# Softmax weights of two batches transposed by TensorE instead of by VectorE and DMAs

## The chip, the cores and the metric

The kernel runs on one core of a Trainium2 chip. The metric is the time of one execution in device microseconds; the number quoted for a kernel is the median of several executions. Besides these there is one execution under the hardware profiler, whose instructions can be read one by one; "the span" is the time from its first to its last instruction.

## What is computed

The input is 64 batches of 128 tokens with 512 features. Each batch goes through one multi-query attention layer and gets the result added:

```python
xn   = layernorm(x, g_in)
q    = (xn @ Wq) * DH**-0.5          # 16 heads of 64
k, v = split(xn @ Wkv)               # one head of 64, shared by all query heads
k, v = concat(null_k, k), concat(null_v, v)      # one extra "null" key
sim  = q @ k.T + concat(null_bias, attn_bias)    # 128 queries x 129 keys
sim  = where(causal or padding mask, -big, sim)
out  = softmax(sim) @ v
x    = x + layernorm(out @ Wo, g_out)
```

All of it is float32.

## The kernel before

The order of the work is written out by hand: the kernel is one long function `step(n)`, called for n = -6 to 62, and each engine executes its own instructions in the order in which `step` issues them. There is no planner. In step n, batch n is at the product of softmax weights and values, batch n+1 at its exponentials, batch n+2 at its scores, batch n-1 at its output projection, and the queries of a group of four later batches are being computed, one quarter per step. Steps up to n = 0 fill this pipeline. The steps that matter here are n = -1, 0 and 1.

**The queries** of groups 1 and later are computed by a scheme with seven products per feature block (`product(g, f, k, ...)`, line 422 in the profile: tiles `pa`, `pw`, `pc`, in PSUM). Products 1, 6, 7 and 4 use the bank `a` one after the other, and ScalarE copies the bank away between them (`keep`, line 433, tiles `kp`, `ku`; `q_out`, line 440 on ScalarE, line 443 on VectorE, tile `qT`). Product 4 and product 3 of a feature block are issued early in the next step (`last`).

**The scores** of a batch (`scores`, line 495, tile `ps`) are computed in two halves: half 0 has the first 64 queries and 64 keys, half 1 has the other 64 queries and 128 keys. Partitions 0 to 63 hold 64 queries of the heads with u = 0, partitions 64 to 127 the same 64 queries of the heads with u = 1, and eight heads lie side by side. The matmuls are 64x64, four of them in the four quarters of the array, and the two halves of its rows write to different banks. Both halves share one two-bank PSUM tile, which is free again when VectorE has added it to bias and mask (`scores_add`, line 508) in the SBUF tile `s`. GpSimd has put bias and mask there before (`bias_add`, line 466; `null_copy`, line 475). There are two such tiles, so batch b+2 takes the one of batch b, and `bias_add(b+2)` waits until batch b's softmax weights have been read for the last time.

**The softmax**: VectorE finds the maxima (line 513), ScalarE computes exponentials and sums head by head (`exps`, line 522), VectorE the reciprocals of the sums (line 539), and GpSimd multiplies by them (`scale`, line 543).

**The transpose.** For the product with the values, the keys have to lie on the partitions. `blocks_T` (line 575) lets VectorE transpose the weights inside blocks of 32x32 into the SBUF tile `sb`, and `blocks_move` (line 601) issues 14 DMAs that carry the blocks to their places in the SBUF tile `aTb`. For all but batch 0 and the last one, the DMAs are issued by SyncE (SP). Batch 0 has its blocks transposed at the end of step -1; 7 of its DMAs are issued by SP there, and 7 by ScalarE in step 0, between the copy `kp` and the addition that `q_out` does. Batch 1 has its blocks transposed in step 0, and its 14 DMAs are issued by SP later in that step, ahead of the four transfers of `tokens_in` (line 295), the loads of `loads_late` and others. `aTb` is shared by all batches but the last eight, and the parts that causality leaves empty were cleared once.

**Values and output**: `values` and `values_end` (line 610, tiles `po`, in the two buffers of the PSUM pool `w`) multiply `aTb` with the values; ScalarE copies the result to SBUF (line 654, tile `oT`). Batch 0 is projected with eight plain matmul steps (`out_mm`, line 669, tile `py`), the following ones in pairs (line 719). `out_stats` computes the output's layer norm.

The PSUM banks `X` and `Y` (pool `ps_y`) belong to the paired output projection. Their first use in the kernel before is in step 2.

The lines around the edits, in step n = 0 and at the end of step n = -1:

```python
product(qg, f, 1, ps_q, "a")
keep("a", "p1")
if n == 0:
    blocks_move(0, take=1)
q_out(qg, f, lo_t, "w", "p1")
```

Of the kernel before, what the change touches and what calls it, by code (L numbers as in the profile page):

```python
# [8 lines left out]
FP = mybir.dt.float32  # L9
# [8 lines left out]
def kernel(  # L18
# [59 lines left out]
    nc = tc.nc  # L78
    B, N, DIM = x.shape
    H = attn_bias.shape[0]  # L80
    DH = w_kv.shape[1] // 2
    P = 128
# [7 lines left out]
    Q = 32  # L90
    NQ = P // Q
    NF = NC // 2
    R8 = 2 * NF
    NL = DH
    ROW = 1 + NL + N + 1
    LK, UK = slice(1, 1 + NL), slice(1 + NL, 1 + NL + N)
# [8 lines left out]
    ps_s = ctx.enter_context(tc.tile_pool(name="ps_s", bufs=1, space=PSUM))  # L105
    ps_q = ctx.enter_context(tc.tile_pool(name="ps_q", bufs=1, space=PSUM))
    ps_y = ctx.enter_context(tc.tile_pool(name="ps_y", bufs=1, space=PSUM))
# [105 lines left out]
    ident = const.tile([P, P], FP, name="ident")  # L213
# [10 lines left out]
    aTb = const.tile([P, 6, R8, Q], FP, name="aTb")  # L224
# [181 lines left out]
    def product(g, f, k, pool, tag, start=True):  # L406

        if start:
            prod[tag] = pool.tile([P, HT], FP, tag=tag, name=f"p{tag}_{g}_{f}_{k}")
        lo, hi = xT[g][:, 0 : GB // 2], xT[g][:, GB // 2 :]  # L410
        t1, t2, t3, t4 = (xS.get((g, i)) for i in range(1, 5))
        w, t = {
            1: (a11, lo[:, :, lo_k]),
            2: (a12, lo[:, :, hi_k]),
            3: (s4, hi[:, :, hi_k]),
            4: (a22, t4),
            5: (s1, t1),
            6: (s2, t2),
            7: (s3, t3),
        }[k]  # L420
        for kc in range(HK):
            nc.tensor.matmul(  # L422
                prod[tag],
                w[:, kc, f * P : (f + 1) * P],
                t[:, :, kc, :],
                start=(start and kc == 0),
                stop=(kc == HK - 1),
                skip_group_check=not start,
            )

    def keep(tag, name):
        kept[name] = bp.tile([P, HT], FP, tag=f"k{name}", name=f"k{name}", bufs=1)
        nc.scalar.copy(kept[name], prod[tag])  # L433

    def q_out(g, c, toks, tag, name=None):
        lo = toks.start // N
        o = q_part(g, c, lo, lo + 2)
        p = prod[tag].rearrange("p (t h i) -> p t h i", t=2, h=2)
        if name is None:
            nc.scalar.copy(o, p)  # L440
        else:
            k = kept.pop(name).rearrange("p (t h i) -> p t h i", t=2, h=2)
            nc.vector.tensor_tensor(o, p, k, ALU.add)  # L443


    S, nmax, rsum = {}, {}, {}
# [13 lines left out]
    def bias_add(b):  # L460
        g, t = divmod(b, GB)
        if b == B3 + 1:
            S[b] = gp.tile([P, R8, ROW], FP, tag="xT", name=f"s_{b}")
        else:
            S[b] = sp.tile([P, R8, ROW], FP, tag="s", name=f"s_{b}")
        nc.gpsimd.tensor_tensor(  # L466
            S[b][:, :, 1 : ROW - 1],
            biasp,
            mneg[g][:, t].unsqueeze(1).broadcast_to([P, R8, NL + N]),
            ALU.add,  # L470
        )

    def null_copy(b):
        g, t = divmod(b, GB)
        nc.gpsimd.tensor_copy(  # L475
            S[b][:, :, 0 : ROW : ROW - 1],
            nv[g][:, t, DH:].rearrange("p (k e) -> p e k", k=2),
        )
# [85 lines left out]
    def aT_of(b):  # L564
        return aTbs[b % 2 if b >= B2 else 0]

    def blocks_T(b):

        if b > B3 and b % 2:
            if not sb2:  # L570
                sb2.append(gp.tile([P, 6, R8, Q], FP, tag="qT", name="sb2"))
            sb = sb2[0]
        else:
            sb = hp.tile([P, 6, R8, Q], FP, tag="sb", name=f"sb_{b}", bufs=1)
        nc.vector.transpose(  # L575
            sb.rearrange("p j e q -> p e j q"),
            S[b][:, :, 1 : ROW - 1].rearrange("p e (j k) -> p e j k", k=Q),
        )
        sbs[b] = sb

    def blocks_move(b, take=None):

        sb = sbs[b] if take == 0 else sbs.pop(b)
        count = 0
        for u in range(2):
            for i in range(2):
                src = slice((2 * u + i) * Q, (2 * u + i + 1) * Q)
                for j in range(3 + i):
                    count += 1
                    if take is not None and count % 2 != take:  # L590
                        continue
                    dst = slice(j * Q, (j + 1) * Q)
                    jL = j - 2 * u
                    jU, iU = 2 + j, 2 + 2 * u + i
                    if 0 <= jL <= i:

                        js, is_ = slice(jL, jU + 1, jU - jL), slice(i, iU + 1, iU - i)
                    else:
                        js, is_ = slice(jU, jU + 1), slice(iU, iU + 1)
                    queue = nc.scalar if take == 1 else nc.sync  # L600
                    queue.dma_start(  # L601
                        out=aT_of(b)[dst, is_].rearrange("p s e q -> p s (e q)"),
                        in_=sb[src, js].rearrange("p s e q -> p s (e q)"),
                    )

    pos = {}

    def value_mm(b, u, half, keys, vals, slots, start=True):
# [54 lines left out]
    def out_mm(b):  # L663
        pool, tag = ps_w, "w"
        if b > P_LAST:
            pool, tag = (ps_q, "c") if b == P_LAST + 2 else (ps_y, "XY"[b % 2])
        py = pool.tile([P, DIM], FP, tag=tag, name=f"py_{b}")
        for c in range(NC):
            nc.tensor.matmul(  # L669
                py, oT[b][:, c, :], wo[:, c, :], start=(c == 0), stop=(c == NC - 1)  # L670
            )
        ys[b] = py
# [21 lines left out]
    def out_sums(p):  # L694

        yS[p] = bp.tile([P, HC, N], FP, tag="yS", name=f"yS_{p}", bufs=1)
        h11, h12 = oT[p][:, lo_c], oT[p][:, hi_c]
        h21, h22 = oT[p + 1][:, lo_c], oT[p + 1][:, hi_c]
        nc.gpsimd.tensor_tensor(yS[p], h21, h22, ALU.add)
        nc.gpsimd.tensor_tensor(h21, h11, h21, ALU.subtract)  # L700
        nc.gpsimd.tensor_tensor(h11, yS[p], h11, ALU.subtract)
        nc.gpsimd.tensor_tensor(h12, h12, h11, ALU.subtract)
# [69 lines left out]
    def out_stats(b):  # L772
        st = small.tile([P, 6], FP, tag="st", name=f"sto_{b}")
        nc.vector.bn_stats(st, ys[b])
        mv = small.tile([P, 2], FP, tag="mvo", name=f"mvo_{b}")
        nc.vector.bn_aggr(mv, st)
        rstd = small.tile([P, 1], FP, tag="rstdo", name=f"rstdo_{b}")
        nc.vector.tensor_scalar(rstd, mv[:, 1:2], EPS, None, ALU.add)
        nc.gpsimd.tensor_tensor(rstd, rstd, nhalf, ALU.pow)
        y = hp.tile([P, DIM], FP, tag="y", name=f"y_{b}", bufs=3)  # L780
        nc.vector.scalar_tensor_tensor(
            y, ys.pop(b), mv[:, 0:1], gob, ALU.subtract, ALU.mult
        )
        if b == B - 1:

            nc.vector.scalar_tensor_tensor(y, y, rstd, res.pop(b), ALU.mult, ALU.add)
        else:
            yr[b] = y, rstd
        ys[b] = y
# [50 lines left out]
    def step(n):  # L840
        def ok(b, end=B):
            return 0 <= b < end
# [4 lines left out]
        q, f = ok(qg, NG), part  # L847
# [17 lines left out]
        nb = n + 2 if n < B3 - 1 else n + 3  # L865
# [5 lines left out]
        if second:  # L871
            if n != B3 + 1:
                out_sums(p5673)
        elif ok(nb) and n >= 0:
            bias_add(nb)
            null_copy(nb)
        if third:
# [18 lines left out]
        if one:  # L896
            out_mm(n - 1)
            if n == 1:
                out_stats(0)
        if fast:  # L900
            if f == 0:
# [80 lines left out]
        if fast:  # L982
            product(qg, f, 1, ps_q, "a")
            keep("a", "p1")
            if n == 0:
                blocks_move(0, take=1)
            q_out(qg, f, lo_t, "w", "p1")
        if soft and not second:
            exps(eb, 1, 6)
# [52 lines left out]
            scores_max(nb, 0)  # L1042
        if one and n > 1:
            out_stats(n - 1)
        if n == 0:
            blocks_T(1)
        if not ok(n) and fast:
            product(qg, f, 6, ps_q, "a", start=False)
            keep("a", "u2")
# [65 lines left out]
        if ok(mk) and not ok(mkv):  # L1115
            kT_out(mk, k_T(mk))
        if n == -1:
            blocks_T(0)
            blocks_move(0, take=0)
        if n == B3 - 2:  # L1120
            bias_add(B3 + 1)
            null_copy(B3 + 1)
# [49 lines left out]
    for n in range(-6, B - 1):  # L1172
        step(n)
        if n == -6:
            for kc in range(2):
                weights_kv(kc)
            for kc in range(2, KC):
                weights_kv_prod(kc)
            load_late()
        if n == -5:  # L1180
            for kc in range(2, KC):
                weights_kv(kc)
            causal(0)
            mask_neg(0)
            weight_sums()
# [49 lines left out]
```

## Time and profile before

| what | value |
|---|---|
| median of 3 executions | 1135.81 us (1134.92 to 1136.13) |
| the profiled execution | 1134.49 us |
| its span | 1132.7 us |
| TensorE (PE) busy, share of the span | 1084.5 us, 96% |
| VectorE (DVE) busy | 807.5 us, 71% |
| GpSimd (POOL) busy | 745.9 us, 66% |
| ScalarE (ACT) busy | 678.5 us, 60% |
| mean granted TensorE clock | 0.995 |
| busiest DMA queue, q1, share of 16 engines | 40.3% |

In the lines of the profile, a number at the start of a line is the time from the span's start in microseconds, and the next one a duration. "PE L610 ... [4.39 <-DMA aTb<-sb]" means that TensorE sat idle for 4.39 us before this instruction of line 610, and that a DMA from `sb` to `aTb` ended the wait. "SPq" and "ACTq" are the instruction queues of SP and ScalarE when they issue DMAs. A float32 matmul is recorded as two instructions, a transpose as one, so a half of scores, 16 matmuls, shows as x32. Matmuls overlap: a group's duration is a little longer than the distance to the start of the next group, and the distance is what counts in a sum.

### The profile page before, as it was taken

The numbers are of one execution on the slowest core, as the hardware profiler recorded it, in microseconds if no ns is written. First come the engines' busy times: TensorE is split into PE (matmuls) and PEld (weight loads), VectorE is DVE, ScalarE is ACT, GpSimd is POOL, SyncE is SP. The second block draws the span as 40 slices with busy tenths as digits, with TensorE's granted clock in tenths as the row PEclk, the third lists the DMA queues.
The fourth block names the chain that finished last, engine by engine and source line by source line (L and its number), as shares of the span: only waits on it lengthen the run. The fifth ranks groups of instructions, "written<-read, shape, count | busy, mean of one in ns | idle before, by whom it ended". The sixth has DMA issues, their size and how long they took to land.

```text
span 1132.7 us, 27381 instructions
## 1 busy us (share of the span) xinstructions
PE 1084.5 (96%) x9700; PEld 869.1 (77%) x9700; DVE 807.5 (71%) x1737; ACT 678.5 (60%) x2710; POOL 745.9 (66%) x588
## 2 busy tenths in 40 slices
PE   6877999999999999999999999999999999999897
PEld 4454788888878888888888888888888888887642
DVE  6563677776787777788777778877777886666762
ACT  2344656566756656675666667666666755657661
POOL 5444877767665676857577686757767675676742
PEclk9998999999999999999999999999999999999999
DMA  6314234353453435335353533534353353422333
GB/s 184 123 37 126 73 123 118 93 167 100 126 127 120 115 98 163 103 125 135 104 135 97 164 106 122 136 116 121 97 164 107 120 136 112 103 73 72 95 97 107
DMA packets 109591, 131.39 MB, mean 116 GB/s; under 512 B 29712, under 2 KB 74256, under 8 KB 107664
## 3 DMA queue, kind: packets, MB, share of 16 engines
q1 hardware_dynamic: 107776, 127.95, 40.3%
q10 hardware_dynamic: 1680, 1.71, 0.5%
q8 instruction: 77, 1.26, 0.5%
q14 instruction: 58, 0.48, 0.1%
HBM read 54.86 MB, written 31.46 MB: 76 GB/s over the span
## 4 chain that ended last, share of the span: by engine, by line
PE 71%; POOL 7%; DVE 6%; DMA 6%; SPq 4%; issue 2%; ACT 2%; ACTq 1%; POOLq 0%; DVEq 0%
PE pa L422 15%; PE pyX L719 14%; PE pc L422 7%; PE ps L495 7%; PE pyY L719 7%; PE po L610 7%; PE pk L308 4%; PE pw L422 4%; PE pyw L719 3%; DMA x<-in_x_dram 3%; SPq L601 3%; PE py L669 2%; POOL s L466 2%; POOL xS L404 1%; POOL s L543 1%
## 5 line engine op out<-in xcount | busy, mean ns | idle before, releaser
L522 ACT ACTIVATE s<-s,nmax 128x65 f32<-128x65 f32 (+1 forms) x1024 | 372.1, 368 | 1.3 <-DVE nmax L513 0.9
L466 POOL TENSOR_TENSOR s<-biasp,mneg 128x1536 f32<-128x1536 f32 x64 | 221.1, 3455 | 108.3 <-DVE sb L575 105.1
L543 POOL TENSOR_TENSOR s<-s,rinv 128x512 f32<-128x512 f32 (+1 forms) x128 | 189.4, 1481 | 125.7 <-DVE nmro L761 88.6
L654 ACT ACTIVATE oT<-po,nv 128x512 f32<-128x512 f32 x128 | 81.1, 684 | 210.9 <-PE po L610 210.9
L522 ACT ACTIVATION_READ_ACCUMULATOR s<-s,nmax 128x1 f32 x1024 | 194.7, 190 | 0.0
L719 PE MATMUL pyX<-wT,oT 128*128 128x256 f32 x696 | 164.6, 379 | 1.1 <-DVE kyu L731 1.1
L719 PEld LDWEIGHTS pyX<-wT,oT 128*128 128x128 f32 x696 | 132.0, 190 | 19.8 <-DVE kyu L731 1.5
L508 DVE TENSOR_TENSOR s<-ps,s 128x512 f32<-128x512 f32 (+1 forms) x128 | 121.4, 949 | 14.8 <-PE ps L495 12.7
L495 PEld LDWEIGHTS ps<-kT,qT 64*64 64x64 f32 x4096 | 93.9, 135 | 46.9 <-DVE s L508 24.5
L422 PE MATMUL pa<-xS,wq 128*128 128x256 f32 x480 | 123.6, 380 | 2.5 <-ACT ku L433 1.5
L513 DVE TENSOR_REDUCE nmax<-s 128x8 f32<-128x520 f32 (+1 forms) x128 | 120.1, 938 | 5.1 <-POOL s L475 3.7
L575 DVE STREAM_TRANSPOSE sb<-s 128x1536 f32<-128x1536 f32 x64 | 113.5, 1773 | 11.8 <-POOL s L543 4.9
L495 PE MATMUL ps<-kT,qT 64*64 64x64 f32 (+1 forms) x4096 | 118.4, 252 | 3.7 <-DVE s L508 2.5
L610 PE MATMUL po<-aTb,vs 64*64 64x256 f32 (+1 forms) x1240 | 116.7, 383 | 1.3 <-DMA aTb<-sb 1.3
L433 ACT COPY ku<-pa 128x256 f32<-128x256 f32 x120 | 44.8, 373 | 93.1 <-PE pa L422 93.1
L422 PEld LDWEIGHTS pa<-xS,wq 128*128 128x128 f32 x480 | 86.8, 190 | 13.1 <-ACT ku L433 2.5
L422 PE MATMUL pc<-xS,wS 128*128 128x256 f32 x240 | 63.3, 386 | 8.3 <-POOL xS L404 7.3
L308 PE MATMUL pk<-wkv,xT 128*128 128x144 f32 x488 | 69.9, 286 | 0.0
L443 DVE TENSOR_TENSOR qT<-pw,kp 128x256 f32<-128x256 f32 x60 | 25.4, 423 | 59.9 <-ACT kp L433 59.8
L422 PE MATMUL pa<-xS,wS 128*128 128x256 f32 x240 | 68.0, 406 | 0.0
L610 PEld LDWEIGHTS po<-aTb,vs 64*64 64x64 f32 (+1 forms) x1240 | 57.5, 135 | 10.9 <-issue 4.6
L308 PEld LDWEIGHTS pk<-wkv,xT 128*128 128x128 f32 x488 | 63.4, 191 | 0.2
(114 smaller groups left out, 2060.7 us busy)
## 6 DMA issues: line engine op xcount, KB each, us to landing
aTb<-sb SPq DMA_DIRECT2D x378, 64.0 KB
x<-in_x_dram SPq DMA_DIRECT2D x64, 256.0 KB
res<-in_x_dram SPq DMA_DIRECT2D x64, 256.0 KB
out_dram<-y SPq DMA_DIRECT2D x64, 256.0 KB
aTb<-sb SPq DMA_DIRECT2D x504, 32.0 KB
xd<-xb SPq DMA_DIRECT2D x14, 1024.0 KB
xT<-xd SPq DMA_DIRECT2D x56, 256.0 KB
wo<-in_L_cond_Wo_dram SPq DMA_DIRECT2D x1, 2048.0 KB
```

The costliest lines, as they stand in the source:

```text
L308: nc.tensor.matmul(pkv, xT[g][:, t, kc, :], wkv[:, kc, :], start=(kc == 0), stop=(kc == KC - 1),)
L422: nc.tensor.matmul(prod[tag], w[:, kc, f * P : (f + 1) * P], t[:, :, kc, :], start=(start and kc == 0), stop=(kc == HK - 1), skip_group_ch ...
L466: nc.gpsimd.tensor_tensor(S[b][:, :, 1 : ROW - 1], biasp, mneg[g][:, t].unsqueeze(1).broadcast_to([P, R8, NL + N]), ALU.add,)
L495: nc.tensor.matmul(pv[u * DH : (u + 1) * DH, r, f, :], qT[g][rows, f, t, hf, u], kT[b][rows, 0:nk], start=True, stop=True,)
L508: nc.vector.tensor_tensor(sv, pss.pop((b, hf)), sv, ALU.add)
L513: nc.vector.tensor_reduce(nmax[b][:, hf], S[b][:, :, WITH_NULL[hf]], AX.X, ALU.max, negate=True)
L522: nc.scalar.activation(row, row, AF.Exp, bias=nmax[b][:, hf, k : k + 1], accum_out=rsum[b][:, hf, k : k + 1],)
L543: nc.gpsimd.tensor_tensor(sv, sv, rinvs.pop((b, hf)).unsqueeze(2).broadcast_to([P, R8, sv.shape[2]]), ALU.mult,)
L575: nc.vector.transpose(sb.rearrange("p j e q -> p e j q"), S[b][:, :, 1 : ROW - 1].rearrange("p e (j k) -> p e j k", k=Q),)
L610: nc.tensor.matmul(pos[b][u][r * DH : (r + 1) * DH, half], vals[keys, b % GB, 0:DH], aT_of(b)[keys, slots, r * NF : (r + 1) * NF], start=s ...
L654: nc.scalar.activation(oT[b][:, u * NF : (u + 1) * NF, :].rearrange("p f (s q) -> p s f q", q=Q), po[u].rearrange("p h i f q -> p (h i) f q"),
L719: nc.tensor.matmul(prod[key], h[:, c, :], w[:, c, :], start=(start and c == 0), stop=(c == HC - 1), skip_group_check=not start,)
```

## The change

A new function `attn_T_pe(b)` takes the place of `blocks_T` and `blocks_move` for batches 0 and 1. TensorE transposes the second half of the weights (64 queries times two groups of heads against 128 keys, eight 128x128 transposes) into the two banks of the scores, and the first half (64 keys, 16 matmuls 64x64 with the identity, which lie in two of the four quarters of the array) into the bank `X`. Three copies by VectorE bring them to `aTb`, each 128 x 512 elements. No DMA is issued.

For batch 0 this is issued at the end of step -1, after product 7 of that step and before product 4 in step 0. For batch 1 it is issued in step 1, after `out_mm(0)` and before product 2 and product 4, which is later than `blocks_T(1)` was. Since the tile of batch 1's weights is now read later, `bias_add(3)` and `null_copy(3)`, which overwrite it, move from the start of step 1 to after the transposes.

```diff
+    def attn_T_pe(b):
+        pu = ps_s.tile([P, 2, NF, N], FP, tag="s", name=f"paU_{b}")
+        for k in range(R8):
+            nc.tensor.transpose(pu[:, k // NF, k % NF, :], S[b][:, k, UK], ident)
+        pl = ps_y.tile([P, R8, DH], FP, tag="X", name=f"paL_{b}")
+        for k in range(R8):
+            for u in range(2):
+                rows = slice(u * DH, (u + 1) * DH)
+                nc.tensor.matmul(
+                    pl[rows, k, :],
+                    S[b][rows, k, LK],
+                    ident[rows, rows],
+                    start=True,
+                    stop=True,
+                )
+        for r in range(2):
+            nc.vector.tensor_copy(
+                aTb[:, 2:, r * NF : (r + 1) * NF, :].rearrange("p s f q -> p f s q"),
+                pu[:, r].rearrange("p f (s q) -> p f s q", q=Q),
+            )
+        nc.vector.tensor_copy(
+            aTb[:, 0:2].rearrange("p s e q -> p e s q"),
+            pl.rearrange("p e (s q) -> p e s q", q=Q),
+        )
...
-        elif ok(nb) and n >= 0:
+        elif ok(nb) and n >= 0 and n != 1:
             bias_add(nb)
             null_copy(nb)
...
             out_mm(n - 1)
             if n == 1:
+                attn_T_pe(1)
+                bias_add(nb)
+                null_copy(nb)
                 out_stats(0)
...
             keep("a", "p1")
-            if n == 0:
-                blocks_move(0, take=1)
             q_out(qg, f, lo_t, "w", "p1")
...
-        if n == 0:
-            blocks_T(1)
...
         if n == -1:
-            blocks_T(0)
-            blocks_move(0, take=0)
+            attn_T_pe(0)
```

## The prediction

> **What bounds the kernel now.** First the page: the engines' busy tenths in 40 slices of 28.3 us.
>
> ```profile
> span 1132.7 us, 27381 instructions
> PE   6877999999999999999999999999999999999897
> PEclk9998999999999999999999999999999999999999
> ```
>
> From the fifth slice on TensorE has nothing to wait for, so what happens there is worth nothing unless it changes TensorE's work. The first four slices (to 113 us) are not full, and the change lies in them. What TensorE wins or loses before it becomes full is carried to the end unchanged, as a shift. So the question is by how much the point shifts at which it becomes full, about 130 us.
>
> Next, who TensorE waited for in the first 130 us (total, times, longest), and in the chain of work that ended last the piece about batch 0's weights (start, duration):
>
> ```profile
> PE po L610 <- DMA aTb<-sb: 5.7, 2, 4.4
> PE po L610 <- DVE qT L443: 1.6, 1, 1.6
> ```
>
> ```profile
> 83.66 0.21 ACTq L601
> ...
> 87.33 4.38 DMA aTb<-sb
> 91.70 0.14 issue
> 91.84 1.34 PE po L610 x9
> ```
>
> ScalarE spends 83.66 to 87.9 on seven DMA issues, the last lands at 91.7, and only then can the values of batch 0 go on. The timelines of ScalarE, GpSimd and TensorE say the same and name what else is late:
>
> ```profile
> 83.14 4.83 ACTq L601 DMA_DIRECT2D aTb<-sb  x7
> 88.02 0.81 ACT L259 ACTIVATE x<-x,nmr,rstd 128x512 f32<-128x512 f32 x1 [4.53 <-DMA aTb<-sb]
> ```
>
> ```profile
> 76.96 1.91 POOL L543 TENSOR_TENSOR s<-s,rinv 128x1024 f32<-128x1024 f32 x1 [3.79 <-DVE rinv L539]
> ```
>
> ```profile
> 78.54 1.13 PE L422 MATMUL pa<-xS,wq 128*128 128x256 f32 x4 [0.52 <-ACT ku L433]
> 91.84 0.69 PE L610 MATMUL po<-aTb,nv 64*64 64x256 f32 x2 [4.39 <-DMA aTb<-sb]
> 99.42 7.03 PE L669 MATMUL py<-wo,oT 128*128 128x512 f32 x16
> 106.28 1.03 PE L422 MATMUL pw<-xT,wq 128*128 128x256 f32 x4
> 113.44 0.43 PE L610 MATMUL po<-aTb,nv 64*64 64x256 f32 x2 [1.64 <-DVE qT L443]
> ```
>
> Batch 0's weights are scaled at 78.87 (76.96 + 1.91). ScalarE's issues hold up its exponentials of batch 1 behind them too. Last, the stages of 1 us: columns are busy us of PE, PEld, DVE, ACT, POOL, then the granted clock, DMA share, GB/s.
>
> ```profile
> 90.00:91.00 1.00, 0.00 (x0) 0.00 (x0) 0.00 (x0) 1.00 (x6) 0.00 (x0) 0.50 0.90 309
> 94.00:95.00 1.00, 1.00 (x25) 1.00 (x20) 1.00 (x3) 0.00 (x0) 1.00 (x2) 0.50 0.06 16
> 115.00:116.00 1.00, 1.00 (x26) 1.00 (x22) 0.19 (x2) 0.49 (x1) 1.00 (x2) 0.50 0.26 99
> ```
>
> After the long stall the clock is at half until about 96.6, and again from 113.9 to 117.2.
>
> **The change, part by part.** *TensorE's added work* is T per batch. The transposes have a row: line 268's four 128x128 transposes took 0.44 us from start to next start in the chain (54.58 to 55.02), so eight take 0.88. The 16 matmuls of 64x64 with 64 columns have a near row: a first half of scores, the same count and shape, took 0.62 (130.31, x32) with all four quarters of the array working, 8 records each, 77 ns a record. Here only two quarters work, 16 records each: 1.24. With about 0.2 for changes of tile shape (my estimate; the step from 64x64 to 128x128 costs 1.06 or 1.13 where a full stream of four takes 0.86), T = 2.3.
>
> Bounds: from below, if the issue and not the quarter sets the pace, 0.62 and T = 1.5. From above the Trainium skill speaks against the change: "TensorEngine Tiling (Array Packing)", section "Gotcha 1: PSUM Pressure", says that different row tiles can't use one PSUM bank at the same time. Here the two row halves write to the one bank `X`; in all of scores and values the row halves write to different banks, so no row here shows the case. By the rule the 32 records go one after the other, 32 x 77 ns = 2.5 us, T about 3.5. They do write to different partitions, so I take the row, and keep 3.5 in the range.
>
> *Batch 0.* TensorE reaches the new work at about 77.8 (product 7 done) and waits for the scaling, until about 78.95, a new stall of 1.1 us. Its queue is in order, so product 4 stands behind it, and behind that ScalarE's copy `qT` and all of batch 1's exponentials. Product 4 starts at 78.95 + 2.3 = 81.25 instead of 78.54. VectorE's three copies of 128x512 out of PSUM cost about 0.6 each (128x128 starts 0.20 apart in line 347, 128x512 takes 0.69 with two inputs in line 508), 1.8 to 2.1 against 1.7 for the removed block transposes: nothing, since VectorE idles 2.0 and 4.5 us soon after. `aTb` is complete near 82.5 and no longer limits.
>
> Now ScalarE is the limit, and I follow it with durations of before. The copy `qT` comes 1.17 after product 4's start (78.54 to 79.71): 82.4. Copy and eight exponentials take 3.04: 85.5. Copy `kp` 0.3, VectorE's `qT` and `nmr` 0.55: 86.3. Then without the seven issues the activation of line 259 (0.72), eight exponentials (3.1, 88.74 to 91.83), two `oT` copies (1.3): 91.5. Copy `ku`, then product 7 of step 0, 0.43 later: 91.9. TensorE meanwhile has four products to 85.6, scores to 86.25, values and the second scores half in 2.45 (130.8 to 133.3, warm), product 6 and the key-value matmuls to 90.9, so it waits 1.0. Product 7 started at 98.55 before: the shift here is 6.6. Product 7 and `out_mm(0)` follow at their own length, 0.87 + 6.87: 99.65, against 106.28.
>
> GpSimd's `bias_add(2)` can start at 81.3, when TensorE has read the weights, instead of 82.42; it is not the limit.
>
> *Batch 1.* Its weights are scaled by about 92, the banks free, so TensorE does not wait: 99.65 + 2.3 = 101.95 where product 2 started at 106.28. The shift falls to 4.3. It can be written as 8.9 - 2T. SP's 14 issues (9.39 us) go. Behind them stood four `xT` transfers, landed at 111.7 and first read at 124.6, and loads: all hidden, worth nothing. VectorE's copies replace the block transposes, with idle time of 4.4 us before `out_stats` as cover; if it were gone, 0.3 us.
>
> *The moved bias.* `bias_add(3)` (3.45) and the null copy now start at 101.9 and end near 105.6. The score addition that needs them comes about 4.3 earlier than 113.95, at 109.6, so 4 us of slack. Queued behind on GpSimd are the power for `out_stats` and the first scaling of batch 2, before at 110.28, now due near 106; it may be 0.3 late and its reader, line 575, waits for the second scaling anyway. Nothing.
>
> *The second stall* (113.44, idle 1.64) stays: it is ScalarE's chain from product 4 through the exponentials of batch 2 to `kp`, and all of that moves together, to 109.1. What is open is the clock. "TensorE: Matmul & The Clock Gate", section "Part 1: The HAM clock gate (the "warmup" mystery)", says that it falls after a whole idle window of some 3.4 us. By that rule 1.64 us never halves it; the trace shows that it did, at 113.9. By the row the shift stays 4.3. By the rule TensorE gains another 1.6 (4.0 us at half clock against 2.4 for the same work at 130.8), but then VectorE's block transpose and additions of batch 2, which come from ScalarE's chain, set the pace through mask, `bias_add(4)` and `xS` to the stall at 129.18, and only about 0.3 is left. So 4.3 to 4.6, and I take 4.4.
>
> Against the profiled execution, 1134.49 (span 1132.7 plus 1.8 around it) becomes 1130.1. That execution is 1.3 below the median, and I put the same shift on the median: 1135.81 - 4.4 = **1131.4 us**.
>
> **Rivals.** A difference under 0.2% (2.3 us) is what a measurement of this kernel can't tell from none.
>
> - *One bank, one row half at a time* (T = 3.5): 8.9 - 7.0 + 0.1 = 2.0 gained, 1133.8. For it the page, against it the different partitions. 10%.
> - *The clock falls at the new stall.* At 76.5 to 81.3 TensorE now idles 1.5 us and then runs partly filled; half clock for 3.4 us of work costs 1.7: 1133.1. For it, the fall at 113.9 after as short a stall; against it, the full products before. 7%.
> - *The shift is given back*, by GpSimd (`bias_add(3)` more than 4 us late) or a later wait: 1135.8. Against it the slack above and a TensorE full from 130 us on; for it the `pc` stalls on `xS` (4.4 us in five after 130 us), which show GpSimd close behind. 6%.
> - *Slower: weight loads not overlapped.* Each 64x64 record needs its own load, 135 ns in line 495. If these go one after the other in the two quarters, 32 x 0.135 = 4.3, T = 5.4 and with it 8.9 - 10.8: 1137.7; with the streaming added as well (64 columns, an eighth of the 0.43 us of one 512-column record of line 669, 54 ns), T = 7.1 and 1141. It decides from T = 4.45 on, 112 ns per record. For it: identity matmuls have 64 columns to hide a load behind. Against it: scores, with the same columns, hide them. 8%.
> - *Cheaper* (T = 1.5): 8.9 - 3.0 = 5.9 and up to 6.2, 1129.8. 7%.
>
> **How the numbers follow.** The forecast has 62%, its own range is 1130 to 1132.8. Faster: forecast, cheaper and clock, 76%. Same: one bank and given back, 16%. Slower: 8%. The range 1129.0 to 1135.0 takes in the bounds of T from 1.5 to 3.5 with the spread of the runs (0.6) on each side, and leaves out given back, slower and tails.
>
> **What would show it.** In the profile of after: TensorE waits about 1.1 us for line 543 near 78 us; line 610 no longer waits for `aTb`; eight transposes in 0.9 and 16 matmuls in 1.3 us; ScalarE's `x` activation near 86; `out_mm(0)` at 92.8; the 1.6 us stall at about 109. Wrong would be: a `paL` group of 2.5 us or more, half clock near 80, line 508 waiting for line 466 near 110, or new waits after 130 us.

## The result, and the profile after

The changed kernel takes 1129.82 us (median of 4 executions, 1129.39 to 1131.5) against 1135.97 us (1134.92 to 1136.99): a ratio of 0.9949 with a 95% interval of 0.9932 to 0.9966. Two more comparisons, each on another chip, gave 0.9954 (0.9939 to 0.9969) and 0.9928 (0.9907 to 0.9949). So it is faster, by 6.2 us in the medians of the first comparison, 5.6 in the second and 7.5 in the third, where 4.4 was forecast. The two executions under the profiler differ by only 3.0 us (1134.49 to 1131.5): the one of before is among the fastest of its kernel, the one of after the slowest of its four.

The page of after:

```profile
span 1129.7 us, 27504 instructions
PE   6988999999999999999999999999999999999887
PEclk9999999999999999999999999999999999999999
```

The second to fourth slices are fuller by a tenth each (9, 8, 8 after 8, 7, 7), and the clock shows no slice under 9 (before, the fourth was at 8). Who TensorE waited for in the first 130 us:

```profile
PE po L636 <- DVE done L668: 2.2, 1, 2.2
...
PE po L636 <- DVE qT L443: 1.7, 1, 1.7
...
PE paU L610 <- POOL s L543: 0.9, 1, 0.9
```

The 5.7 us of waiting for `aTb` are gone. 0.9 us of waiting for the scaling are there instead, close to the forecast 1.1, and 2.2 us that were not forecast. TensorE's timeline of after:

```profile
77.55 1.13 PE L422 MATMUL pa<-xS,wq 128*128 128x256 f32 x4 [0.47 <-ACT ku L433]
79.58 1.09 PE L610 MATMUL paU<-ident,s 128*128 128x128 f32 x8 [0.90 <-POOL s L543]
80.60 1.15 PE L615 MATMUL paL<-ident,s 64*64 64x64 f32 x32
81.68 1.13 PE L422 MATMUL pa<-xS,wq 128*128 128x256 f32 x4
...
91.00 0.66 PE L636 MATMUL po<-aTb,vs 64*64 64x256 f32 x8 [2.20 <-DVE done L668]
...
94.52 7.03 PE L695 MATMUL py<-wo,oT 128*128 128x512 f32 x16
...
103.43 1.13 PE L422 MATMUL pw<-xT,wq 128*128 128x256 f32 x4
...
110.72 0.64 PE L636 MATMUL po<-aTb,nv 64*64 64x256 f32 x2 [1.66 <-DVE qT L443]
...
126.46 1.13 PE L422 MATMUL pc<-xS,wS 128*128 128x256 f32 x4 [0.98 <-POOL xS L404]
```

The first and the last line bound the stretch in which the edits lie: from product 7 of step -1 (the work just ahead of the transposes) to product 5 of step 2, from which on TensorE is full. In the timeline of before they are:

```profile
76.89 1.13 PE L422 MATMUL pa<-xS,wq 128*128 128x256 f32 x4 [0.45 <-ACT ku L433]
129.18 1.13 PE L422 MATMUL pc<-xS,wS 128*128 128x256 f32 x4 [0.97 <-POOL xS L404]
```

So the stretch takes 48.9 us (126.46 - 77.55) after and 52.3 (129.18 - 76.89) before. These 3.4 us are the difference in this pair of profiles. The stretch is the measure for what follows, because it leaves out what differs by chance before and behind it. It differs by chance too, but less: two more profiles of before gave 52.4 and 51.1 us, two more of after 48.9 and 50.1. So a pair differs by 1.0 to 3.5 us, and the means of three by 2.6. What moves a single profile is mostly where the clock falls, as the parts on the clock below show.

The granted clock in stages of after (columns as before):

```profile
43.00:44.00 1.00, 1.00 (x6) 1.00 (x5) 0.00 (x0) 0.80 (x2) 1.00 (x1) 0.50 0.00 0
90.00:91.00 1.00, 0.00 (x0) 0.00 (x0) 0.28 (x3) 0.69 (x4) 0.00 (x0) 1.00 0.66 119
111.00:112.00 1.00, 1.00 (x13) 0.52 (x7) 0.88 (x3) 0.66 (x1) 0.69 (x1) 0.50 0.00 0
```

At 90 us, where the clock was at half in before, it is full. At 111 it falls behind the second stall, as in before. At 43 it fell in this execution of after and not in that of before. It fell between 42 and 47 us in six of the ten profiles with an edit of the change, and in none of the other four. Nothing in the code differs there, so I take it for chance ahead of the stretch, but the runs don't settle it.

### The profile page after: what moved, and what is told of

Read it like the earlier page. It is cut to its first block, busy times and chain, and to the rows that moved or that the text cites. A ratio compares the mean times of both kernels' runs of the same rounds, so it can differ in the third digit from the quotient of the medians.

```text
span 1129.7 us, 27504 instructions
## 1 busy us (share of the span) xinstructions
PE 1087.6 (96%) x9780; PEld 872.5 (77%) x9780; DVE 809.5 (72%) x1741; ACT 680.8 (60%) x2710; POOL 745.8 (66%) x588
## 3 DMA queue, kind: packets, MB, share of 16 engines
q10 hardware_dynamic: 1248, 1.38, 0.4%
## 4 chain that ended last, share of the span: by engine, by line
PE 71%; DVE 7%; DMA 7%; POOL 6%; SPq 4%; ACT 3%; issue 2%; POOLq 0%; DVEq 0%; ACTq 0%
PE pa L422 15%; PE pyX L745 14%; PE pc L422 7%; PE ps L495 7%; PE pyY L745 7%; PE po L636 6%; DMA x<-in_x_dram 5%; PE pk L308 4%; PE pw L422 3%; PE py L695 3%; PE pyw L745 3%; SPq L601 2%; ACT s L522 2%; POOL s L543 1%; POOL s L466 1%
## 5 line engine op out<-in xcount | busy, mean ns | idle before, releaser
L575 DVE STREAM_TRANSPOSE sb<-s 128x1536 f32<-128x1536 f32 x62 | 110.0, 1774 | 11.5 <-POOL s L543 4.6
L246 POOL TENSOR_TENSOR rstd<-rstd,nhalf 128x1 f32<-128x1 f32 x64 | 35.9, 561 | 43.3 <-DVE rstd L245 43.3
```

Source lines behind the costliest of these rows:

```text
L575: nc.vector.transpose(sb.rearrange("p j e q -> p e j q"), S[b][:, :, 1 : ROW - 1].rearrange("p e (j k) -> p e j k", k=Q),)
```

## The experiments

Twelve runs, with the two first profiles, and their stretch. "Time" is the ratio to the kernel before on the same chip with its 95% interval; intervals are some 4 us wide, so a difference of 1 or 2 us is read from the stretch and not from the time.

| run | stretch, us | time, ratio (interval) |
|---|---|---|
| before / before_2 / before_3 | 52.3 / 52.4 / 51.1 | |
| after / after_again / after_3 | 48.9 / 48.9 / 50.1 | 0.9949 / 0.9954 / 0.9928 |
| pe0_only | 47.2 | 0.9955 (0.9939 to 0.9971) |
| pe1_only | 54.9 | 1.0008 (0.9994 to 1.0023) |
| done_first | 47.9 | 0.9953 (0.9936 to 0.9970) |
| pe0_done | 47.3 | 0.9952 (0.9934 to 0.9970) |
| best | 46.6 | 0.9958 (0.9943 to 0.9972) |
| halves_in_turn | 50.0 | 0.9965 (0.9950 to 0.9980) |
| sp_only | 52.6 | 1.0025 (1.0007 to 1.0042) |
| loads_first | 48.8 | 1.0041 (1.0022 to 1.0060) |

### Which batch brings the gain: pe0_only and pe1_only

pe0_only undoes the change for batch 1, pe1_only for batch 0:

```diff
# pe0_only, against after
-                attn_T_pe(1)
-                bias_add(nb)          # back at the start of step 1
-                null_copy(nb)
+        if n == 0:
+            blocks_T(1)               # and blocks_move(1) with it
# pe1_only, against after
-            attn_T_pe(0)
+            blocks_T(0)
+            blocks_move(0, take=0)    # and take=1 in step 0
```

> Batch 0 by TensorE as in the change, batch 1 by VectorE and 14 DMAs of SP as before. Theory A (the whole gain is batch 0's: the landing of its last DMA and the issues on ScalarE; batch 1's DMAs were hidden and its transposes only cost TensorE 2.1 us): about 2 us faster than after_again, some 8 under before. Rival B (both batches gain, by DMAs and issues that go): slower than after_again by 2 us or more. Between them: batch 1's DMAs, issued about 5 us earlier than before and needed about 5 us earlier too, become late and TensorE waits for line 601's transfers at values of batch 1; then within 1 us of after_again.

> Batch 0 by DMAs as before, 7 of them issued by ScalarE, batch 1 by TensorE as in the change. Theory A: slower than before by the 2.1 us of TensorE's work, 1138; TensorE still waits 4.4 us for the DMAs of batch 0. Rival B: faster than before by 2 us or more.

TensorE in pe1_only:

```profile
92.24 0.69 PE L636 MATMUL po<-aTb,nv 64*64 64x256 f32 x2 [4.36 <-DMA aTb<-sb]
...
132.19 1.13 PE L422 MATMUL pc<-xS,wS 128*128 128x256 f32 x4 [0.96 <-POOL xS L404]
```

Its stretch is 54.9 us, 2.6 longer than before: the wait for batch 0 is all there, and batch 1's transposes, 2.0 us of TensorE (106.80 to 108.84 in this run), come on top. Its time isn't shorter than before; its interval takes in the expected 2.1 us more as well as no difference. TensorE in pe0_only:

```profile
100.20 1.03 PE L422 MATMUL pw<-xT,wq 128*128 128x256 f32 x4
...
107.36 0.43 PE L636 MATMUL po<-aTb,nv 64*64 64x256 f32 x2 [1.63 <-DVE qT L443]
...
123.61 1.13 PE L422 MATMUL pc<-xS,wS 128*128 128x256 f32 x4 [2.28 <-POOL xS L404]
```

Its stretch is 47.2 us, 1.7 shorter than in after, and no line of it waits for batch 1's DMAs. So in the stretch theory A holds: batch 0 brings all of the gain, and batch 1 gives a part of it back. The time does not show it: it is that of after (0.9955 beside 0.9954) and not the expected 2 us less. In its profile TensorE loses another 2.1 us behind the stretch, at boundaries of groups (below), and pe0_done 2.3; best, which also has batch 1 on DMAs, loses nothing there, so the runs can't tell whether this is chance.

Nor do all of the 2.1 us arrive within the stretch: TensorE comes to product 5 earlier and waits 2.28 us for `xS` in place of 0.98. The cause lies with GpSimd, which stood still for the residual of batch 0 before it came to `bias_add(4)` and `xS`:

```profile
112.89 1.27 POOL L822 TENSOR_TENSOR y<-y,res 128x512 f32<-128x512 f32 x1 [3.04 <-DMA res<-in_x_dram]
114.11 2.36 POOL L718 TENSOR_TENSOR wT<-wo,wT 128x1024 f32<-128x1024 f32 x1
117.10 3.45 POOL L466 TENSOR_TENSOR s<-biasp,mneg 128x1536 f32<-128x1536 f32 x1 [0.63 <-DVE mneg L452]
```

SP issues that load at 104.91, behind batch 1's 14 DMAs (from 93.60, for 9.21 us) and four `xT` transfers. In after, without the 14, it is issued at 91.27 and GpSimd does not wait for it. VectorE's mask, which line 466 needs, was then not done in time either: its first instruction of line 452 took 1.20 us (0.29 in after) and ended some 0.15 us after GpSimd's line 718. From the start of line 452 to line 466 it took 1.68 us (115.42 to 117.10) in place of 0.76 (119.18 to 119.94), so this chain costs about 0.9 us here. Another part of the longer wait is the clock, which fell behind the second stall in after and not in pe0_only.

### The new stall: done_first

VectorE's timeline of after just ahead of the unforeseen wait:

```profile
90.72 0.20 DVE L539 RECIPROCAL rinv<-rsum 128x8 f32<-128x8 f32 x1 [3.07 <-ACT s L522]
90.84 0.11 DVE L668 COPY done<-po 128x1 f32<-128x1 f32 x1
```

TensorE's second part of the values waits for `done`, a copy of one column that VectorE makes from the first part. The first part was finished at about 88. But VectorE works in order, and ahead of `done` stood the reciprocals of batch 1's second half, which wait for ScalarE's last exponential. In before, VectorE was through with those reciprocals at about 92, ahead of the end of the first part, and `done` (93.85) waited for TensorE.

```diff
-            if ok(n + 1) and fill:
+            if ok(n + 1) and fill and n < 0:
                 rinv(n + 1, 1)
                 scale(n + 1, 1)
         ...
             values(n, split)
+        if n == 0:
+            rinv(1, 1)
+            scale(1, 1)
```

> The changed kernel, but in step 0 the reciprocals and the scaling of batch 1's second half are issued after the first half of the values, so that VectorE's small copy (done) that the second half of the values waits for is not behind the reciprocals, which wait for ScalarE. Theory A (the 2.20 us that TensorE waited for done in the profile of after is a new stall that the prediction missed, in the place of the 1.0 us that it expected at product 7): TensorE waits at product 7 of step 0 for ScalarE instead, about 1 us, and the kernel is about 1 us faster than after_again. Rival (the stall has slack behind it, since ScalarE's chain sets the pace): within 0.3 us of after_again.

TensorE in done_first:

```profile
89.26 0.61 PE L636 MATMUL po<-aTb,vs 64*64 64x256 f32 x8
...
91.93 0.33 PE L342 MATMUL pk<-ident,ktok 128*128 128x128 f32 x1 [0.99 <-ACT oT L680]
```

The stall is gone, and 0.99 us of waiting for ScalarE come a little later, at the transpose of the keys (which takes over a buffer of the pool `w` from the values) and not at product 7. The stretch is 47.9 us, 1.0 shorter. That is the expected effect; in the time it can't be seen.

### Two halves of the array and one bank: halves_in_turn

```diff
-        for k in range(R8):
-            for u in range(2):
+        for u in range(2):
+            for k in range(R8):
```

> The changed kernel, with the 16 identity matmuls in another order: first the eight of the upper row half, then the eight of the lower. In the profile of after they alternate and take 1.08 us for 32 records. Theory A (both row halves worked at the same time, writing to one bank): now each half works alone, 16 records at some 67 ns and again 16, so 2.1 us per batch, and the kernel is 2 us slower than after_again. Rival D (the halves never overlapped, each record takes 34 ns by itself because both share a bank): 1.08 us again and the same time.

```profile
81.50 1.90 PE L615 MATMUL paL<-ident,s 64*64 64x64 f32 x32
83.33 1.13 PE L422 MATMUL pa<-xS,wq 128*128 128x256 f32 x4
```

In turn, the 32 records take 1.83 us from start to next start; alternating (after, 80.60 to 81.68) 1.08. That is 57 ns a record against 34. The streaming of 64 columns alone takes some 54 ns, an estimate from `out_mm(0)` (16 records of 512 columns in 6.87 us, an eighth of one). So at 34 ns a record two halves of the array's rows did work at the same time, writing to different partitions of one bank; it isn't just that a weight load is hidden. The gain is 1.7-fold, not quite double. The stretch grew by 1.1 us, less than twice 0.75; in this run the clock did not fall behind the second stall, as it did in after.

### Landing or issues: sp_only

```diff
-            blocks_move(0, take=0)
+            blocks_move(0)            # all 14 issued by SP
...
-            if n == 0:
-                blocks_move(0, take=1)
```

> The kernel before with one edit: all 14 DMAs of batch 0 are issued by SP in step -1, none by ScalarE. Theory A (TensorE's 4.4 us wait is for the landing of the last block, and ScalarE's issues only shorten it): SP needs 14 x 0.66 = 9.3 us from 82.4, so the last block lands 2 to 4 us after 91.7, and TensorE's wait for line 601's transfers is 6 to 8 us in all in place of 5.7; slower than before by 2 to 4 us although ScalarE is free 4.8 us earlier. Rival C (the seven issues on ScalarE are what costs, since batch 1's exponentials stand behind them): faster than before by 2 us or more.

In sp_only TensorE waits 7.0 us for batch 0's blocks (5.7 before), the longer wait being:

```profile
92.99 0.69 PE L610 MATMUL po<-aTb,nv 64*64 64x256 f32 x2 [5.13 <-DMA aTb<-sb]
```

ScalarE's last exponential of batch 1 ends 1.2 us earlier (90.62 for 91.83), and nothing is won by it, so rival C falls: the landing of the last block set the pace. The wait is 1.3 us longer, and yet the stretch grew by only 0.3 us. The clock makes up the rest: in this execution it did not fall behind the second stall, as it did in before. Beside before_3, where it did not fall there either, the stretch is 1.5 us longer. Of the expected 2 to 4 us in the time, 2.8 came (0.25%), but most of them from behind the stretch, where this profile lost 5.4 us more than that of before, and they are not shown to be due to the edit. What ScalarE's issues would cost with the landing out of the way was not measured.

### Putting it together: best and pe0_done

best joins pe0_only and done_first and moves batch 0's transposes behind product 4:

```diff
         if last:
             product(last_g, last_f, 4, ps_q, "a", start=False)
+        if n == 0:
+            attn_T_pe(0)
+            bias_add(nb)              # no longer at the start of step 0
+            null_copy(nb)
...
-        if n == -1:
-            attn_T_pe(0)
```

> Three edits to the changed kernel: batch 1 by VectorE and DMAs as before (pe0_only), the reciprocals after the values (done_first), and batch 0's transposes behind product 4 of step 0 instead of ahead of it, with bias_add(2) and null_copy(2) moved behind them, so that ScalarE's copy of product 4 and the exponentials of batch 1 no longer stand behind the wait for the scaling. The stretch of TensorE from product 7 of step -1 to product 5 of step 2 was 52.3 us in before, 48.9 in after, 47.2 in pe0_only, 47.9 in done_first. Theory A (what is won there arrives at the end, but for chance): the stretch is 45 to 46 us and the time 3 us under after_again. Rival E (a second limit stands behind TensorE after 130 us: at each boundary of a group of four, loads of x and of nulls land late, because SP issues them behind four large transfers of tokens_in, and GpSimd and TensorE wait for them; then what is won earlier is given back there): the stretch is as short, but the time is within 1 us of after_again, and TensorE's waits for xS (line 404) after 130 us are 5 us or more, where before has 4.4 and after 2.9 to 4.3.

TensorE in best:

```profile
78.56 1.13 PE L422 MATMUL pa<-xS,wq 128*128 128x256 f32 x4 [0.52 <-ACT ku L433]
79.53 1.04 PE L610 MATMUL paU<-ident,s 128*128 128x128 f32 x8
...
123.54 1.81 PE L422 MATMUL pc<-xS,wS 128*128 128x256 f32 x4 [2.64 <-POOL xS L404]
```

The wait for the scaling is filled by product 4, and the stretch is 46.6 us, not the expected 45 to 46. Yet the time isn't better than that of after (0.9958, on another chip). TensorE waits 2.64 us for `xS` at the end of the stretch, and the clock falls behind that wait: the group takes 1.81 us in place of 1.13. Rival E expected 5 us or more of waiting for `xS` after 130 us; in this profile it is 3.4 us.

> Two of the edits of best on the changed kernel: batch 1 by VectorE and DMAs as before, and the reciprocals after the values; batch 0's transposes stay where the change has them. Theory A: the stretch to product 5 of step 2 is between 46.3 (what best has) and 47.2 us (pe0_only). By the limit that GpSimd sets there (TensorE waited 2.28 us for xS in pe0_only and 2.64 in best) most of the 0.9 us of done_first is not to be had again: 47 us, and a time within 1 us of pe0_only.

It showed the same limit: 47.3 us (best measured 46.6, not the 46.3 of the expectation), a wait of 2.67 us for `xS`, half clock behind it. Of the 1.0 us that done_first won on after, nothing is left here. The limit is the one of pe0_only, and stronger, as in best:

```profile
112.81 1.27 POOL L822 TENSOR_TENSOR y<-y,res 128x512 f32<-128x512 f32 x1 [4.24 <-DMA res<-in_x_dram]
```

```profile
114.59 2.29 DVE L452 TENSOR_SCALAR mneg<-m 128x256 f32<-128x256 uint8 x2
```

From the start of line 452 to line 466 it takes 2.43 us in best and 2.47 in pe0_done, 1.7 more than in after, which is the difference of the waits for `xS` (2.64 and 2.67 in place of 0.98). So by these traces what bounds the start of the kernel from here on is again a DMA, the residual that SP issues behind batch 1's blocks. A kernel that issues it earlier was not run. No version was shown to beat after.

### Behind the stretch: before_2, before_3, after_again, after_3, loads_first

> The changed kernel once more, for a second profile and more times. The profiled execution of after had two stretches at half clock that the one of before lacks, at 42 to 46 us and at about 1097 us, and they cost it 1.25 and 1.7 us of work. Theory A (the shift is the steps of the prediction, with the chance of the clock on top): 4.4 to 6.5 us under before in the medians, and a profile without these two stretches has a span of about 1127.5 to 1128.5. Rival (the change itself brings the slow stretches): the second profile has them at the same places, span near 1129.7.

> The kernel before, unchanged, for a second profile of it. Its profiled execution (1134.49 us, mean clock 0.995) was faster than nearly all others of before, whose mean clock lies between 0.989 and 0.995, while executions of after lie between 0.995 and 1.0. Theory F (the part of the measured difference above the 3.4 us that the two profiles show up to 130 us is TensorE's clock, which falls more often in before): the stretch from product 7 of step -1 to product 5 of step 2 is again 52 to 54 us, and with a lower mean clock this execution shows more stretches at half clock than the first profile, each with some 1.7 us lost behind a wait at a boundary of a group of four. Rival A (chance of the head, before 63 us): the stretches behind 130 us are as in the first profile, and the difference lies ahead of 63 us.

> The kernel before, unchanged, for a third profile. As for before_2.

> The changed kernel, unchanged, for a third profile and for times beside those of before on the same chip. Theory F: the stretch to product 5 of step 2 is 48.9 us again where the clock falls behind the second stall (at 110 us), 48 to 48.9 where it does not; the time 4.4 to 6.5 us under before, the more the lower the clock of before was.

The stretch of before_2 was as expected, that of before_3 (51.1) shorter, that of after_3 (50.1) longer, and the time of after_3 is 7.5 us under before, more than the 6.5 expected. after_again has the fall of the clock at 43 us again and none near 1097; its span, 1129.3 us, is above the 1127.5 to 1128.5 expected of theory A for a profile with neither.

The comparison of one transpose per step (line 342, 61 in all) between two profiles shows where a shift comes or goes. It stays constant within 0.1 us over most steps and jumps by 0.1 to 2.7 us, up or down, at some of the boundaries between groups of four batches. From the end of the stretch to the last of these transposes, the profiles of before differ by up to 5.0 us among themselves (0, +5.0, +0.9), those of after by 1.6 (-0.6, 0.0, +1.0, all against the first of before). Not all of it is chance. In all profiles with both edits but loads_first (after, after_again, after_3, done_first, halves_in_turn) TensorE is another 3.3 to 3.7 us ahead of before at the transpose that before has at 467.66 us, and loses most or all of it again up to the last; no other profile is more than 0.8 ahead there. Why is open. TensorE's wait for `xS` after 130 us in before, and then in before_2, the same kernel:

```profile
PE pc L422 <- POOL xS L404: 4.4, 5, 1.8
```

```profile
PE pc L422 <- POOL xS L404: 9.6, 11, 1.3
```

What makes GpSimd late at a boundary is seen in pe0_only, where one boundary cost 2.7 us (up to 1.7 of them by the clock, which was at half from about 457.8 to 461); VectorE, then GpSimd, then TensorE:

```profile
451.01 0.69 DVE L241 BATCH_NORM_STATS2 st<-x 128x6 f32<-128x512 f32 x1 [1.93 <-DMA x<-in_x_dram]
```

```profile
451.53 0.21 POOL L475 COPY s<-nv 128x16 f32<-128x16 f32 x1 [3.76 <-DMA nv<-vs]
```

```profile
457.08 1.50 PE L422 MATMUL pc<-xS,wS 128*128 128x256 f32 x4 [1.90 <-POOL xS L404]
```

SP issued that load of `x` and the move of `nv` behind the four `xT` transfers of 256 KB, and they landed late. loads_first lets SP issue the loads ahead of those transfers:

```diff
+        if n < B3:
+            transfers()
         if (n + 8) % GB == 0 and 2 <= (n + 8) // GB < NG:
             tokens_in((n + 8) // GB)
-        if n < B3:
-            transfers()
```

> The changed kernel with one more edit: in the steps with tokens_in (line 295), the loads of x and of the residual (loads_late) are issued by SP ahead of the four transfers, not behind. Rival E (the waits at group boundaries come from the late load of x): VectorE no longer waits there for x, TensorE's waits for xS after 130 us fall from 2.9 to 4.3 us to under 2, the kernel is 1.5 to 4 us faster than after_again and its times spread less. Theory A alone (those waits come from GpSimd's own work and are chance): the same time within 1 us, or slower if xT is late for product 2.

Its waits after 130 us:

```profile
PE po L636 <- DMA aTb<-sb: 8.2, 7, 1.7
...
PE pc L422 <- POOL xS L404: 1.0, 2, 0.6
```

VectorE no longer waits for `x` (3.1 us in after), and the waits for `xS` fall to 1.0 us (2.9 in after). That fits the late load as their cause. It is no proof, for TensorE now waits elsewhere, which gives GpSimd time: softmax blocks land late, seven times, which costs more (8.2 us), and the kernel is slower than before by 0.4%. Times did not spread less (1136.1 to 1145.6). In this kernel the order of issue chose who waits for the burst of transfers at a boundary.

The clock: in the executions of the second comparison the median of the mean granted clock was 0.993 for before (25 executions) and 0.9975 for after (10). The first profile of before accounts for three windows of 3.4 us at half clock (two behind the 4.4 us stall, one behind the second), 5.1 us of clock lost; the difference of medians is 5.1 us of clock too (0.0045 x 1133), of which the two windows at the removed stall are 3.4. So a typical execution of before would have about one half-clock window more than its profiles, or one of after one fewer, worth up to 1.7 us. Theory F is supported by these means, but weakly. No profile caught that window: before_2 and before_3 have three windows as well (one of before_3's lies at 61 us, ahead of the stretch), the three profiles of after have three, two and two. And the mean is not sharp: with the same three windows it reads 0.995, 0.994 and 0.994 in the profiles of before, and 0.001 is 1.1 us. Where the rest of the difference arises is open.

## Why the prediction was right

**The point, the place and the mechanism.** Batch 0's blocks no longer come by DMA, and TensorE's wait for them is gone. pe0_only and pe1_only show that it was this wait: the gain comes and goes with batch 0's edit alone. The range held 1129.82, and the forecast missed by 1.6 us. By its number alone the result is that of the rival "cheaper" (1129.8), outside the forecast's own range of 1130 to 1132.8; but that rival had T = 1.5, which was not met.

**TensorE's added work** was forecast at T = 2.3 and took 2.1 (79.58 to 81.68) and 2.05 us (101.38 to 103.43). The row (two quarters at 77 ns a record, 1.24) was near the measured 1.08; the eight transposes took 1.0 in place of 0.88. By the rule on one bank (the Trainium skill, "TensorEngine Tiling (Array Packing)", section "Gotcha 1: PSUM Pressure") the 16 matmuls would have taken 2.5 by the forecast's estimate. The rivals with T = 3.5 and over fall. The rule did not hold here, for writes to different partitions. A slip in the sum of the rival on weight loads has no bearing: T = 4.45 is 105 ns a record, not 112, with its own 0.2 for changes of tile shape.

**Batch 0's step.** The wait for the scaling was forecast at 1.1 and took 0.9. ScalarE's activation of line 259 was expected near 86.3:

```profile
86.77 0.82 ACT L259 ACTIVATE x<-x,nmr,rstd 128x512 f32<-128x512 f32 x1 [0.61 <-DVE nmr L258]
```

This execution was 0.66 us later from the start, so it is right. Then a step failed: "so it waits 1.0", the wait at product 7 for ScalarE. The chain of VectorE was followed for `qT` and `nmr` only; that `done` stands behind the reciprocals was overlooked. The wait was 2.2 us, and came earlier. Product 2 of step 1 started 25.9 us after product 7 of step -1 (103.43 - 77.55), where the forecast had 25.1 (101.95 - 76.89) and before 29.4: a shift of 3.5 and not 4.3. done_first wins 1.0 us in the stretch by taking that wait away.

**Batch 1.** The forecast had the shift fall by T there, from 6.6 to 4.3, since batch 1's DMAs were hidden; it fell from 5.6 to 3.5. pe0_only and pe1_only show the cost, with 1.7 and 2.6 us of stretch. The moved bias was worth nothing, as forecast: the score addition of batch 3 (line 508, at 111.22) did not wait for `bias_add(3)`. That SP's 14 issues and the loads behind them are worth nothing holds beside before, where pe1_only wins nothing by taking them away. It does not hold once batch 0's wait is gone: in pe0_only, best and pe0_done they make the residual late, for 0.9 to 1.7 us.

**The second stall and the clock.** The stall stayed, 1.66 us, and the clock fell behind it in after and after_again, so the row was right against the rule that the forecast weighed against it, by which it falls after a whole idle window of some 3.4 us (the Trainium skill, "TensorE: Matmul & The Clock Gate", section "Part 1: The HAM clock gate (the "warmup" mystery)"). In after_3, halves_in_turn and before_3 it did not fall there; the wait for `xS` that follows was then 1.37 to 1.38 us in place of 0.96 to 0.98, and from the end of the stall to product 5 it took 15.3 us in place of 15.7 (before, after). So 0.4 us of what TensorE won arrived, where the forecast had about 0.3. In after_3 it fell behind the new stall instead:

```profile
89.48 0.66 PE L636 MATMUL po<-aTb,vs 64*64 64x256 f32 x8 [2.17 <-DVE done L668]
90.08 2.08 PE L422 MATMUL pa<-xS,wS 128*128 128x256 f32 x4
91.95 0.42 PE L342 MATMUL pk<-ident,ktok 128*128 128x128 f32 x1
92.16 1.78 PE L308 MATMUL pk<-wkv,xT 128*128 128x144 f32 x8
```

From the end of that stall to product 7 it took 4.3 us, in after 2.65 (91.00 to 93.65). This is the rival "the clock falls at the new stall", at another stall than the one named.

**"I put the same shift on the median"** was too simple, and is the second term that was mis-sized. The stretch is shorter by 3.4 us in the first pair of profiles and by 2.6 in the means of three, less than the forecast 4.4, and the medians differ by 5.6 to 7.5, which is more. Perhaps 1.7 of the rest is the clock, by the means of the second comparison; what is left is within what the boundaries of groups shift. Behind it stand two readings that don't hold: that TensorE has nothing to wait for from the fifth slice on (for `xS` alone it waits 4.4 us after 130 us in the first profile of before and 9.6 in before_2), and that a shift is carried to the end unchanged. That the forecast is as near as it is is luck: it comes from two errors of opposite sign.

## What to carry to other kernels

Where a bound engine waits for a DMA late in the pipeline's filling, doing that transfer's work on the engine itself pays once for each batch that waits, and costs its full time for each batch that doesn't: here one batch of the two. A transfer that was hidden need not stay so once the wait ahead of it is gone: look at what is queued behind it. When a stall is removed, look at every engine in order for the instruction that the next release hangs on, even one of 0.1 us, and at what stands ahead of it in that queue. And a shift in one profile isn't the shift of the median: take a stretch bounded by the same instructions in both profiles, and count the half-clock windows that a removed stall takes with it.

## What the runs showed of the hardware that was not expected

- The clock fell to half behind stalls of 1.6 to 2.7 us, in some executions and not in others with the same stall: behind the same 1.64 us it fell in before and not in before_3. Each of these falls lasted about 3.4 us, and the one at the 4.4 us wait of before twice that.
- With TensorE full, two executions of the same program (before_2 against before) still differed by 5.0 us behind the stretch, in jumps at boundaries of groups. Where one jump was followed (pe0_only, 2.7 us), the late landing of one 256 KB load and of a small move behind four transfers of the same queue was at its start.
- Two matmuls of 64x64 in different halves of the array's rows overlapped although both wrote to one PSUM bank, to different partitions: 34 ns a record alternating (after), 57 in turn (halves_in_turn).
- VectorE's first instruction of line 452, 0.29 us in after, took 1.20 to 1.99 us while GpSimd ran line 718, and ended some 0.15 us after it (pe0_only, best, pe0_done). What ties the two is not shown.
